# The scan's B held as three bf16 pieces and spread over the partitions by one bf16 product per state

## The chip, the cores and the metric

The kernel runs on one core of a Trainium2 chip. The metric is the time of one launch on the device in microseconds (us); lower is better. Several executions are timed, and one more is recorded by the hardware profiler.

## The reference, cut to what matters

The program is a two-layer network on x of shape (8, 512, 256) in float32. Each layer normalises x and adds two branches to it. In layer 0 the branches are a Mamba block (a selective state-space scan) and an FFN whose activations and weights are rounded to four-bit values in blocks of 16; in layer 1 they are a block-sparse attention and a two-deep stack of local attention and FFN. The change concerns the Mamba block:

```python
u = silu(conv(x_in) + conv_b)                        # (batch, 512 tokens, 512 channels)
x_dbl = einsum('bld,ed->ble', u, W_xproj)            # 16 + 16 + 16 columns
delta_raw, B_ssm, C_ssm = x_dbl[..., :16], x_dbl[..., 16:32], x_dbl[..., 32:]
delta = softplus(einsum('blr,dr->bld', delta_raw, W_dt) + b_dt)
def step(h, inp):                                    # over the tokens
    d_t, u_t, B_t, C_t = inp
    h = exp(d_t[:, :, None] * A) * h + (d_t * u_t)[:, :, None] * B_t[:, None, :]
    return h, einsum('bdn,bn->bd', h, C_t)           # 16 states n
```

Then y = ys + D u is gated with silu(z) and projected back to 256 columns. B at one token and one state is a single number which all 512 channels need.

## The kernel before, in words

The kernel has two stages, one for each layer, and the second begins when the first is over. In both, channels lie on the 128 partitions and the 512 tokens of one batch along them, so that a token scan is one VectorE (DVE) instruction along a row. NC = 4 groups of 128 channels make up the 512 channels, NS = 16 is the number of states, KC = 2 the groups of the 256 model columns, NB = 8 the batches.

The first stage is built from generators. `head(b)` (L251) loads and normalises a batch, turns it with TensorE (PE), runs the input projection and the convolution (L264 to L275), projects u to the 48 rows of delta, B and C (`ps_xp`, L279), copies them from PSUM to the tile `xd` with ScalarE (ACT, L283), writes the 16 rows of C to DRAM (L285), and forms delta and du = delta * u (L294 to L305: one PE product, four ACT operations, two DVE operations and three GpSimd (POOL) operations for each group of channels). `ffn(b)` (L309) is the four-bit FFN: rounding in `fp4` (L81 to L109), gate and up products (L330, L336), the turn of the hidden rows (`inner_to_partitions`, L191) and the down product (L350).

`scan(b)` (L356) is the recurrence. For each half of the channels (two groups, c0) and each of the 16 states n it does one step:

- a DMA from SP's queue spreads C's row n over the partitions (`cb`, L363, three buffers);
- a PE product spreads B's row n over the partitions: `sel[:, n, :]` has ones in row 16 + n and zeros elsewhere, so that `sel.T @ xd` repeats that row of `xd` 128 times in PSUM (`bb`, L366, pool `pb` of two buffers);
- for each of two channel groups: hh = du * bb (DVE, L369), da = exp(delta * A) (ACT, L374), the scan along the tokens (DVE, L376), hh * cb (POOL, L377), and a PE product with the identity that adds hh to `y` in PSUM over the 16 states (L378).

After the 16 states, z is projected and gated (L384 to L393), and after both halves the output projection (L399) and the sum (L403) close the batch.

`beside` (L111) interleaves the steps of `scan(b)` with those of `ffn(b)` and `head(b + 1)`; the first batch also carries the rounding of the weights and two tables. This gives the order in which the program is written. A scheduler of the framework then orders the instructions of each engine at compile time, by costs of its own, and within an engine the order is fixed when the program runs. Buffers that rotate (`rot`: `h` six, `cb` three; `pmm`, `pb`, `pda` two each in PSUM) set how far one engine may run ahead of another.

`sel` is made once at the start by 16 DVE copies of a column of the identity (L176 to L179), and `w_xp` and `w_dt` are loaded at L165 and L166.

Of the kernel before, what the change touches and what calls it, by code (L numbers as in the profile page):

```python
# [9 lines left out]
FP = mybir.dt.float32  # L10
BF = mybir.dt.bfloat16
AF = mybir.ActivationFunctionType
ALU = mybir.AluOpType
# [4 lines left out]
P = 128  # L18
NB, L, D = 8, 512, 256
NT = L // P  # L20
KC = D // P
DI, NS, DR = 512, 16, 16
NC = DI // P
# [7 lines left out]
DEPTH = 2  # L31
HID = 682
NHC = (HID + P - 1) // P
EPS = 1e-5
MASKED = -1e30

# [2 lines left out]
def tile_kernel(ctx: ExitStack, tc: tile.TileContext, a: dict, out: bass.AP):  # L39
    nc = tc.nc  # L40
    pe, dve, act, pool, sp = nc.tensor, nc.vector, nc.scalar, nc.gpsimd, nc.sync
# [87 lines left out]
    ident = const.tile([P, P], FP, name="ident")  # L129
# [4 lines left out]
    def load(p, src, shape, name, eng=sp):  # L134
        t = p.tile(shape, FP, name=name)
        eng.dma_start(t, src)
        return t

    def chunks(w):
        return w.rearrange("(k p) n -> p k n", p=P)  # L140
# [4 lines left out]
    with ExitStack() as s0:  # L145
        w0 = s0.enter_context(tc.tile_pool(name="w0", bufs=1))
        w1 = s0.enter_context(tc.tile_pool(name="io0", bufs=2))
# [14 lines left out]
        w_in = load(w0, chunks(a["w_in"]), [P, KC, 2 * DI], "w_in")  # L162
        conv_w = load(w0, a["conv_w"], [P, NC, 4], "conv_w")
        conv_b = load(w0, a["conv_b"], [P, NC], "conv_b")
        w_xp = load(w0, chunks(a["w_xp"]), [P, NC, DR + 2 * NS], "w_xp")  # L165
        w_dt = load(w0, a["w_dt"], [DR, DI], "w_dt")  # L166
        b_dt = load(w0, a["b_dt"], [P, NC], "b_dt")
        a_neg = load(w0, chunks(a["a_log"]), [P, NC, NS], "a_neg")
        d_par = load(w0, a["d_par"], [P, NC], "d_par")
# [2 lines left out]
        dve.tensor_scalar(a_neg, a_neg, -1.0, None, ALU.mult)  # L172


        sel = w0.tile([DR + 2 * NS, NS, P], FP, name="sel")
        for n in range(NS):  # L176
            dve.tensor_copy(
                sel[:, n, :], ident[: DR + 2 * NS, DR + n : DR + n + 1].to_broadcast([DR + 2 * NS, P])
            )  # L179


        w_g = w0.tile([P, KC, FI], FP, name="w_g")
# [66 lines left out]
        made = {}  # L249

        def head(b):  # L251
            x = load_x(b)
            xn = w1.tile([P, NT, D], FP, tag="xn", name="xn")
            layernorm(x, xn, sm)
            xt = w1.tile([P, KC, L], FP, tag="xt", name="xt")
            to_channels(xn, xt, pmm, "mm")
            yield


            u = w1.tile([P, NC, L], FP, tag="u", name="u")  # L260
            for c in range(NC):
                ps = pmm.tile([P, L], FP, tag="mm", name="ps_in")
                for k in range(KC):
                    pe.matmul(  # L264
                        ps, w_in[:, k, c * P : (c + 1) * P], xt[:, k, :], start=(k == 0), stop=(k == KC - 1)
                    )
                cv = rot.tile([P, L], FP, tag="t0", name="cv")
                dve.tensor_scalar(
                    cv, ps, conv_w[:, c, 3:4], conv_b[:, c : c + 1], ALU.mult, ALU.add
                )  # L270
                for s in range(1, 4):
                    dve.scalar_tensor_tensor(
                        cv[:, s:], ps[:, : L - s], conv_w[:, c, 3 - s : 4 - s], cv[:, s:], ALU.mult, ALU.add
                    )
                act.activation(u[:, c, :], cv, AF.Silu)  # L275
                yield
            ps = pmm.tile([P, L], FP, tag="mm", name="ps_xp")
            for c in range(NC):
                pe.matmul(  # L279
                    ps[: DR + 2 * NS, :], w_xp[:, c, :], u[:, c, :], start=(c == 0), stop=(c == NC - 1)  # L280
                )
            xd = w1.tile([DR + 2 * NS, L], FP, tag="xd", name="xd")
            act.copy(xd, ps[: DR + 2 * NS, :])  # L283
            c_d = dram.tile([NS, L], FP, tag="c_d", name="c_d")
            sp.dma_start(c_d, xd[DR + NS :, :])  # L285
            yield

            delta = w1.tile([P, NC, L], FP, tag="delta", name="delta")  # L290
            du = w1.tile([P, NC, L], FP, tag="du", name="du")
            for c in range(NC):
                ps = pmm.tile([P, L], FP, tag="mm", name="ps_dt")
                pe.matmul(ps, w_dt[:, c * P : (c + 1) * P], xd[:DR, :], start=True, stop=True)  # L294
                e = rot.tile([P, L], FP, tag="t0", name="e")
                w = rot.tile([P, L], FP, tag="t1", name="w")
                act.activation(e, ps, AF.Abs, bias=b_dt[:, c : c + 1])
                act.activation(delta[:, c, :], ps, AF.Relu, bias=b_dt[:, c : c + 1])
                act.activation(e, e, AF.Exp, scale=-1.0)
                dve.tensor_scalar(w, e, 1.0, None, ALU.add)  # L300
                dve.scalar_tensor_tensor(e, w, 1.0, e, ALU.subtract, ALU.subtract)
                act.activation(w, w, AF.Ln)
                pool.tensor_tensor(w, w, e, ALU.subtract)
                pool.tensor_tensor(delta[:, c, :], delta[:, c, :], w, ALU.add)
                pool.tensor_tensor(du[:, c, :], delta[:, c, :], u[:, c, :], ALU.mult)  # L305
                yield
            made[b] = x, xn, xt, u, xd, c_d, delta, du

        def ffn(b):  # L309

# [44 lines left out]

        def scan(b):  # L356

            x, xn, xt, u, xd, c_d, delta, du = made[b]
            for c0 in range(0, NC, 2):
                ys = [py.tile([P, L], FP, tag=f"y{i}", name=f"y{i}") for i in range(2)]  # L360
                for n in range(NS):
                    cb = rot.tile([P, L], FP, tag="cb", name="cb")
                    sp.dma_start(cb, c_d[n].unsqueeze(0).to_broadcast([P, L]))  # L363

                    bb = pb.tile([P, L], FP, tag="bb", name="bb")
                    pe.matmul(bb, sel[:, n, :], xd, start=True, stop=True)  # L366
                    hs = [rot.tile([P, L], FP, tag="h", bufs=6, name="hh") for i in range(2)]
                    for i in range(2):
                        dve.tensor_tensor(hs[i], du[:, c0 + i, :], bb, ALU.mult)  # L369
                    for i in range(2):  # L370
                        c = c0 + i

                        da = pda.tile([P, L], FP, tag="da", name="da")
                        act.activation(da, delta[:, c, :], AF.Exp, scale=a_neg[:, c, n : n + 1])  # L374
                        hh = hs[i]
                        dve.tensor_tensor_scan(hh, da, hh, 0.0, ALU.mult, ALU.add)  # L376
                        pool.tensor_tensor(hh, hh, cb, ALU.mult)  # L377
                        pe.matmul(ys[i], ident, hh, start=(n == 0), stop=(n == NS - 1))  # L378
                    yield
                for i in range(2):  # L380
                    c = c0 + i
                    ps = pmm.tile([P, L], FP, tag="mm", name="ps_z")
                    for k in range(KC):
                        pe.matmul(  # L384
                            ps, w_in[:, k, DI + c * P : DI + (c + 1) * P], xt[:, k, :],
                            start=(k == 0), stop=(k == KC - 1),
                        )
                    z = rot.tile([P, L], FP, tag="t1", name="z")
                    act.activation(z, ps, AF.Silu)
                    dve.scalar_tensor_tensor(  # L390
                        u[:, c, :], u[:, c, :], d_par[:, c : c + 1], ys[i], ALU.mult, ALU.add
                    )
                    pool.tensor_tensor(u[:, c, :], u[:, c, :], z, ALU.mult)  # L393
                yield
            xs = sums.pop(b)
            for t in range(NT):
                ps = pmm.tile([P, L], FP, tag="mm", name="ps_o")
                for c in range(NC):
                    pe.matmul(  # L399
                        ps[:, :D], u[:, c, t * P : (t + 1) * P], w_o[:, c, :],  # L400
                        start=(c == 0), stop=(c == NC - 1),
                    )
                dve.tensor_tensor(xs[:, t, :], xs[:, t, :], ps[:, :D], ALU.add)  # L403
            act.dma_start(x1_d[b], xs)
# [11 lines left out]
    with ExitStack() as s1:  # L416
        w0 = s1.enter_context(tc.tile_pool(name="w1", bufs=1, reuse_waits="tile"))
        w1 = s1.enter_context(tc.tile_pool(name="io1", bufs=2, reuse_waits="tile"))
# [40 lines left out]
        for j in range(4):  # L459
# [4 lines left out]
            "wqkv": [P, KC, 3 * IN], "tab": [P, 4, NT, LD], "wo": [P, IN // P, D],  # L464
            "wf1": [P, KC, 2 * HID], "wf2": [P, NHC, D],
        }
        lng, lnb, b1, b2c = [], [], [], []
        for l in range(DEPTH):
            lng.append(load(w0, a["lng"][l], [P, KC], f"lng{l}"))
            lnb.append(load(w0, a["lnb"][l], [P, KC], f"lnb{l}"))  # L470
            b1.append(load(w0, a["b1"][l], [P, 2, NHC], f"b1{l}"))
            b2c.append(load(w0, a["b2c"][l], [P, KC], f"b2c{l}"))
# [456 lines left out]
        for b in range(NB):  # L929
            more = b + 1 < NB  # L930
# [94 lines left out]
```

## Time and profile before

| | us |
|---|---|
| median of three runs | 4067.3 |
| the three runs | 4056.5, 4067.3, 4068.8 |
| the profiled execution | 4060.3 |
| its span, first to last instruction | 4058.3 |
| first stage | 0 to about 1722 |
| second stage | from there to the end |

Busy time in the whole span: PE 3690.3 us, DVE 2647.0 us, ACT 1724.7 us, POOL 1326.4 us. In the page, a group's row has the line of the kernel, the engine, the operation, what it writes and reads by the program's names, the shape, the count, then the busy time in us and the mean in ns of one, then the idle time of the engine just before the group's instructions and what ended most of it. PEld is PE's weight load, which may run beside a product. "PEclk" is the share of full speed that the PE clock was granted[...].

### The profile page before, as it was taken

How to read it: one execution, taken by the hardware profiler on the slowest of the kernel's cores; microseconds unless marked ns; L12 is line 12 of the kernel's file. 1: busy time of each engine (PE TensorE's matmuls, PEld its weight loads, DVE VectorE, ACT ScalarE, POOL GpSimd, SP SyncE). 2: the span in 40 equal slices, each digit the busy share in tenths (PEclk: the TensorE clock that was granted, in tenths of full speed). 3: DMA queues.
4: the chain of work that ended last, by engine and by line, in shares of the span. 5: the costliest groups of instructions: out<-in, count | busy, mean ns of one | idle time of the engine just before them, and what ended most of it. 6: DMA issues, size and time to landing. Idle time of an engine off the chain costs nothing.

```text
span 4058.3 us, 41394 instructions
## 1 busy us (share of the span) xinstructions
PE 3690.3 (91%) x14428; PEld 1757.7 (43%) x14444; DVE 2647.0 (65%) x4809; ACT 1724.7 (42%) x3411; POOL 1326.4 (33%) x1059
## 2 busy tenths in 40 slices
PE   5889898898988988989999999999999999999998
PEld 1334343434343434344553554544544445445545
DVE  7877879787978787765654555555455456456444
ACT  3454646455645555433343243244234234333333
POOL 4555556555655555521012012021111101201210
PEclk7788789888988888989999999999989999999999
DMA  2111111111111111120011011011101111100100
GB/s 84 45 39 47 45 47 50 44 47 44 47 47 46 49 39 47 60 88 27 27 53 42 14 56 43 20 45 43 38 27 43 38 40 34 53 27 27 48 27 6
DMA packets 88712, 171.96 MB, mean 42 GB/s; under 512 B 10024, under 2 KB 41768, under 8 KB 88504
## 3 DMA queue, kind: packets, MB, share of 16 engines
q1 hardware_dynamic: 85568, 162.95, 12.5%
q10 hardware_dynamic: 2936, 6.36, 0.4%
q8 instruction: 115, 1.88, 0.2%
q14 instruction: 93, 0.76, 0.1%
HBM read 159.58 MB, written 9.70 MB: 42 GB/s over the span
## 4 chain that ended last, share of the span: by engine, by line
PE 46%; DVE 7%; issue 2%; ACT 2%; POOL 1%; DMA 0%; SPq 0%; POOLq 0%; DVEq 0%; ACTq 0%
PE ps_qkv L707 8%; PE ps_g L877 5%; PE ps_a L877 4%; PE ps_wo L839 3%; PE ps_qk L538 3%; PE ps_y L912 2%; PE ps_w L895 2%; PE ps_st L633 2%; PE lo L811 2%; PE pt_qk L698 2%; PE ps_ls L759 2%; DVE pr L788 2%; PE pt L797 1%; DVE nm L769 1%; PE ps_s L583 1%
## 5 line engine op out<-in xcount | busy, mean ns | idle before, releaser
L377 POOL TENSOR_TENSOR hh<-hh,cb 128x512 f32<-128x512 f32 x512 | 660.3, 1302 | 452.3 <-PE y L378 116.8
L378 PE MATMUL y<-hh,ident 128*128 128x512 f32 x1024 | 640.5, 740 | 126.3 <-POOL hh L377 123.5
L376 DVE TENSOR_TENSOR_SCAN hh<-da,hh 128x512 f32<-128x512 f32 x512 | 604.9, 1206 | 11.2 <-ACT da L374 11.1
L374 ACT ACTIVATE da<-delta,a_neg 128x512 f32<-128x512 f32 x512 | 348.7, 689 | 441.1 <-DVE hh L376 439.6
L378 PEld LDWEIGHTS y<-hh,ident 128*128 128x128 f32 x1024 | 202.5, 223 | 460.1 <-POOL hh L377 341.7
L369 DVE TENSOR_TENSOR hh<-du,bb 128x512 f32<-128x512 f32 x512 | 333.9, 672 | 71.7 <-PE bb L366 63.1
L366 PE MATMUL bb<-xd,sel 48*128 48x512 f32 x512 | 311.0, 710 | 26.6 <-DVE hh L369 26.6
L775 ACT ACTIVATE pr<-ps_ls,nm 128x256 f32<-128x256 f32 (+1 forms) x512 | 221.8, 446 | 174.9 <-DVE nm L769 174.7
L726 POOL TENSOR_TENSOR r<-r,r 128x512 f32<-128x512 f32 x128 | 162.8, 1272 | 355.4 <-DVE r L724 355.4
L884 DVE SCALAR_TENSOR_TENSOR ht<-ps_a,b,gl 128x512 f32<-128x512 f32 x96 | 71.9, 749 | 252.1 <-PE ps_a L877 252.1
L487 POOL MEMSET sa<- 128x1 f32 x16 | 1.6, 102 | 711.9 <-DVE sa L843 384.6
L722 DVE TENSOR_TENSOR r<-ps_qkv,tab 128x512 f32<-128x512 f32 x128 | 87.9, 687 | 222.1 <-ACT sq L721 222.1
L883 ACT ACTIVATE gl<-ps_g,b 128x512 f32<-128x512 f32 x96 | 65.9, 686 | 379.4 <-PE ps_g L877 379.4
L877 PE MATMUL ps_g<-hn,wf 128*128 128x512 f32 (+1 forms) x384 | 207.6, 659 | 20.5 <-issue 20.4
L721 ACT ACTIVATE sq<-ps_qkv 128x512 f32<-128x512 f32 x128 | 76.6, 598 | 272.9 <-PE ps_qkv L707 272.9
L877 PE MATMUL ps_a<-hn,wf 128*128 128x512 f32 (+1 forms) x384 | 191.2, 618 | 0.0
L366 PEld LDWEIGHTS bb<-xd,sel 48*128 48x128 f32 x512 | 89.5, 207 | 234.6 <-DVE hh L369 94.6
L637 ACT ACTIVATE pt_e<-ps_st 128x512 f32<-128x512 f32 (+1 forms) x384 | 172.8, 536 | 14.6 <-PE ps_st L631 13.8
L769 DVE TENSOR_REDUCE nm<-ps_ls 128x2 f32<-128x512 f32 (+1 forms) x256 | 147.4, 617 | 43.4 <-PE ps_ls L759 42.6
L707 PE MATMUL ps_qkv<-wqkv,s 128*128 128x512 f32 x384 | 174.9, 605 | 0.0
L707 PE MATMUL ps_qkv<-wqkv,sf 128*128 128x512 f32 x384 | 173.3, 601 | 0.0
L788 DVE TENSOR_SCALAR pr<-pr,lrs 128x256 f32<-128x256 f32 (+1 forms) x512 | 148.6, 332 | 4.8
(213 smaller groups left out, 6622.1 us busy)
## 6 DMA issues: line engine op xcount, KB each, us to landing
cb<-c_d SPq DMA_DIRECT2D x256, 256.0 KB, 3.1
wqkv<-in_wqkv SPq DMA_DIRECT2D x16, 1536.0 KB, 6.2
wf<-in_wf SPq DMA_DIRECT2D x16, 1364.0 KB, 11.0
wf<-in_wf SPq DMA_DIRECT2D x16, 768.0 KB, 4.7
tab<-tab SPq DMA_DIRECT2D x18, 512.0 KB, 6.9
wo<-in_wo SPq DMA_DIRECT2D x16, 512.0 KB, 3.9
x<-in_x SPq DMA_DIRECT2D x8, 512.0 KB, 4.0
x<-xs ACTq DMA_DIRECT2D x8, 512.0 KB, 2.8
```

Of the source, the lines that this page charges most:

```text
L366: pe.matmul(bb, sel[:, n, :], xd, start=True, stop=True)
L369: dve.tensor_tensor(hs[i], du[:, c0 + i, :], bb, ALU.mult)
L374: act.activation(da, delta[:, c, :], AF.Exp, scale=a_neg[:, c, n : n + 1])
L376: dve.tensor_tensor_scan(hh, da, hh, 0.0, ALU.mult, ALU.add)
L377: pool.tensor_tensor(hh, hh, cb, ALU.mult)
L378: pe.matmul(ys[i], ident, hh, start=(n == 0), stop=(n == NS - 1))
L637: act.activation(pt[:, :n], banks[g][:, :n], AF.Exp)
L707: pe.matmul(ps, shifted(s, k, t * P, P), wqkv[:, k, i * IN : (i + 1) * IN], start=(k == 0), stop=(k == KC - 1),)
L769: dve.tensor_reduce(nm, banks[r][:, : 2 * nk].rearrange("p (g n) -> p g n", g=2), AX.X, ALU.max, negate=True)
L775: act.activation(pr[:, at], banks[r][:, at], AF.Exp, bias=nm[:, i : i + 1], accum_out=rs[:, i : i + 1],)
L788: dve.tensor_scalar(pr[:, at], pr[:, at], rs[:, i : i + 1], None, ALU.mult)
L877: pe.matmul(dst[:m], wf1[:, k, off + c * P : off + c * P + m], hn[:, k, :], start=(k == 0), stop=(k == KC - 1),)
```

## The change

The projection `w_xp` is widened on the host from 48 to 128 columns: B's 16 columns stand three times, at rows 0, 64 and 96 of its product, delta's at row 32, C's at row 48. In `head`, `xd` becomes the whole 128-row product in float32, and a bf16 tile `bp` gets its first rounding. Then for rows from 64 on, and again for rows from 96 on, the rounding is subtracted from `xd` on POOL and the rest is rounded into `bp` on ACT. After that the rows at 0, 64 and 96 of `bp` hold three bf16 pieces whose sum is B. `sel` is bf16, with ones at rows n, 64 + n and 96 + n, so that one product adds the three pieces and spreads the sum. The dt product and C's DMA read their rows at their new places. `scan` takes `bp` in the place of `xd`.

```diff
+RD, RC, PIECES = 32, 48, (0, 64, 96)
...
-        w_xp = load(w0, chunks(a["w_xp"]), [P, NC, DR + 2 * NS], "w_xp")
-        w_dt = load(w0, a["w_dt"], [DR, DI], "w_dt")
+        w_xp = load(w0, chunks(a["w_xp"]), [P, NC, P], "w_xp")
+        w_dt = w0.tile([RD + DR, DI], FP, name="w_dt")
+        sp.dma_start(w_dt[RD:, :], a["w_dt"])
...
-        sel = w0.tile([DR + 2 * NS, NS, P], FP, name="sel")
+        sel = w0.tile([P, NS, P], BF, name="sel")
+        every = w0.tile([P, NS], BF, name="every")
+        dve.tensor_copy(every, ident[:, :NS])
+        for at in PIECES[1:]:
+            dve.tensor_tensor(every, every, ident[:, at : at + NS], ALU.add)
         for n in range(NS):
-            dve.tensor_copy(
-                sel[:, n, :], ident[: DR + 2 * NS, DR + n : DR + n + 1].to_broadcast([DR + 2 * NS, P])
-            )
+            dve.tensor_copy(sel[:, n, :], every[:, n : n + 1].to_broadcast([P, P]))
...
             for c in range(NC):
-                pe.matmul(
-                    ps[: DR + 2 * NS, :], w_xp[:, c, :], u[:, c, :], start=(c == 0), stop=(c == NC - 1)
-                )
-            xd = w1.tile([DR + 2 * NS, L], FP, tag="xd", name="xd")
-            act.copy(xd, ps[: DR + 2 * NS, :])
+                pe.matmul(ps, w_xp[:, c, :], u[:, c, :], start=(c == 0), stop=(c == NC - 1))
+            xd = w1.tile([P, L], FP, tag="xd", name="xd")
+            act.copy(xd, ps)
             c_d = dram.tile([NS, L], FP, tag="c_d", name="c_d")
-            sp.dma_start(c_d, xd[DR + NS :, :])
+            sp.dma_start(c_d, xd[RC : RC + NS, :])
+
+            bp = w1.tile([P, L], BF, tag="bp", name="bp")
+            act.copy(bp, ps)
+            for at, more in ((PIECES[1], True), (PIECES[2], False)):
+                pool.tensor_tensor(xd[at:, :], xd[at:, :], bp[at:, :], ALU.subtract)
+                act.copy(bp[at:, :], xd[at:, :])
             yield
...
-                pe.matmul(ps, w_dt[:, c * P : (c + 1) * P], xd[:DR, :], start=True, stop=True)
+                pe.matmul(ps, w_dt[RD:, c * P : (c + 1) * P], xd[RD : RD + DR, :], start=True, stop=True)
...
-            made[b] = x, xn, xt, u, xd, c_d, delta, du
+            made[b] = x, xn, xt, u, bp, c_d, delta, du
...
-            x, xn, xt, u, xd, c_d, delta, du = made[b]
+            x, xn, xt, u, bp, c_d, delta, du = made[b]
...
-                    pe.matmul(bb, sel[:, n, :], xd, start=True, stop=True)
+                    pe.matmul(bb, sel[:, n, :], bp, start=True, stop=True)
...
+    w_xp, xp = i["L0_attn_W_xproj"].T, np.zeros((DI, P), f)
+    xp[:, RD : RD + DR], xp[:, RC : RC + NS] = w_xp[:, :DR], w_xp[:, DR + NS :]
+    for at in PIECES:
+        xp[:, at : at + NS] = w_xp[:, DR : DR + NS]
...
-        "w_xp": i["L0_attn_W_xproj"].T,
+        "w_xp": xp,
```

## The prediction

> **What bounds the kernel now.** I read the busy shares by stage first, because the change touches only the first stage (0 to 1722 us; the last output product of its scan ends there and the second stage begins).
>
> ```profile
> 0.00:1722.00 1722.00, 1496.20 (x3419) 626.64 (x3420) 1397.35 (x1989) 904.11 (x1178) 972.16 (x763) 0.86 0.16 48
> 1024.00:1033.00 9.00, 8.78 (x27) 4.45 (x26) 6.82 (x10) 7.46 (x9) 4.99 (x4) 1.00 0.16 44
> 1066.00:1080.00 14.00, 11.94 (x22) 3.59 (x20) 14.00 (x20) 7.89 (x10) 5.68 (x5) 0.90 0.07 20
> 1690.00:1712.00 22.00, 20.73 (x41) 6.33 (x40) 21.57 (x25) 8.78 (x13) 15.02 (x13) 1.00 0.26 72
> ```
>
> Columns: stretch, length, busy us of PE, PEld, DVE, ACT, POOL, then the granted PE clock. In the whole stage PE is busy 87% and DVE 81%: neither is full. The three short stretches say why. In 1024:1033 (gate and up products of the FFN) PE is full and DVE 76%; in 1066:1080 (convolution beside the scan) DVE is 100% and PE has gaps; in 1690:1712 (scan nearly alone) DVE is 98%. The bound alternates. The groups tell what the scan step costs each engine:
>
> ```profile
> L377 POOL TENSOR_TENSOR hh<-hh,cb 128x512 f32<-128x512 f32 x512 | 660.3, 1302 | 452.3 <-PE y L378 116.8
> L378 PE MATMUL y<-hh,ident 128*128 128x512 f32 x1024 | 640.5, 740 | 126.3 <-POOL hh L377 123.5
> L376 DVE TENSOR_TENSOR_SCAN hh<-da,hh 128x512 f32<-128x512 f32 x512 | 604.9, 1206 | 11.2 <-ACT da L374 11.1
> L369 DVE TENSOR_TENSOR hh<-du,bb 128x512 f32<-128x512 f32 x512 | 333.9, 672 | 71.7 <-PE bb L366 63.1
> L366 PE MATMUL bb<-xd,sel 48*128 48x512 f32 x512 | 311.0, 710 | 26.6 <-DVE hh L369 26.6
> ```
>
> There are 256 steps (8 batches, 2 halves, 16 states), yet bb has x512 and y x1024: one float32 product is two matmul instructions. DVE waits for bb itself only 63.1 us. The row of bb alone, with its waits:
>
> ```profile
> L366 PE MATMUL bb<-xd,sel x512: 589/589/1220, 43.6 to 1708.9; 48*128 48x512 f32 x171
> who waited for it (us, times):
>   POOL hh L377: 70.3, 31
>   DVE hh L369: 63.1, 48
> ```
>
> The median 589 ns is a record with its latency; the timeline has four of them in 1.98 us at full clock, so they follow each other at (1.98 - 0.589)/3 = 0.46 us. Records reach 1220 ns when the clock is halved. The page's chain of waits goes back only to about 1682 us (PE 46% of the span, nearly all second stage). I followed the stage's own waits further back by the same rule, from 1722 to 98 us: of 1624 us PE has 662, DVE 520, "issue" 160, POOL 141, ACT 106, and **bb 118.5**, y 267.
>
> [...]the granted clock is 1 or 0.5, its stretches in this stage are multiples of 3.41 us, and 495 of 1722 us are at half. [...]The trace of before has one such form, the bf16 mask product of the second stage, with a mean record of 391 ns[...].
>
> **The change, part by part.**
>
> *bb in one bf16 product (L366).* A float32 product takes two instructions at about 0.43 to 0.46 us, that is 0.88 us; the bf16 one 0.216[...]. It saves 0.66 us at full clock, 1.3 at half; at the stage's clock of 0.86, 0.77 us, times 256 = 197 us of PE time. That is not the gain. On the chain bb holds 118.5 us, and shrinking it takes off at most 118.5 x (1 - 0.39/1.12) = 77 us: 1.12 us is the pair in the timeline, 0.39 one bf16 record. Since the end is the longest of many paths, a shorter bb can only uncover others: 77 is the upper bound with this order and this clock. What is late next is DVE. When PE is full, DVE is busy 74 to 77% (below), so it takes over only after a fifth of the time is gone, while PE's work falls by about 197/1496 = 13%. But in the fullest stretches (1024:1033) no bb runs at all, and its relief there comes only from a PE queue that arrives earlier. I take 0.7 of the bound, **-54 us**; ends: -25 (a third, only half of the direct wait of 63 us gone) and -77.
>
> *The clock.* [...]I cut the stage into its 3.41 us windows and took PE's streaming share and DVE's busy share in each. Of 343 full-clock windows after 100 us 65 were followed by half clock: 38 of the 49 with a streaming share below 0.6, 15 of 69 between 0.6 and 0.8, one of 218 above. Shares 14% lower move windows down these bins; with the same rate per bin I count about 97 drops instead of 65, and half-clock windows go from 29% to some 38% of the stage, 45 more. Their price: DVE is busy 0.83 on average in half-clock windows against 0.81 in the others, so nothing is lost on average; but in the 32 of them where PE streams over 0.9, DVE is at 0.66, 0.19 of the pace or 0.63 us a window lower. Between 0 and 45 x 0.63 = 28 us; I take the middle, **+14 us**.
>
> *Order.* The scheduler orders by costs of its own. The compiled order of PE differs in about 350 lines of some 8460, mostly y against bb; of DVE in about 790 of 4810; of SP in a few cb and x loads that move by up to six places. No operation is lost. ACT gets 21 more table loads. I take no gain and no loss from the order, **0, within +-20 us**: each half of a step is 3.4 us on DVE, so 20 us is six displaced steps.
>
> *The split into pieces (L278 to L286), per batch.* ACT: the copy of xd now 128 partitions high (578 ns before at 48[...]), and three more copies at 0.58 us; POOL: two subtractions at about 1.3 us (row of L377). Eight batches: ACT 24 x 0.58 = 14 us plus 21 x 1.283 = 27 us, POOL 16 x 1.3 = 21 us. ACT works 904 of 1722 us and is on the chain for 106, a weight of 0.12; POOL 972 and 141, 0.15. So 41 x 0.12 + 21 x 0.15 = **+8 us**; ends 0 and 62. Queued behind them: on ACT the exps of da (for which the scan waits 11.1 us now), on POOL the products hh, for which y waits 123.5 us now. The new wait is bb's for bp: the first bb of the next batch stands on PE ahead of the last ps_dt and two or more pairs of y. Its cover is the time from ps_xp to there, about four scan steps or 14 us, against 4 x 0.58 + 2 x 1.3 = 5 us of chain and perhaps two foreign hh on POOL; if that cover went, it would cost some 5 us a batch, 40 us. dt reads other rows of xd and the compiled order shows it waiting for ACT alone.
>
> *Projection (L279), dt (L294), C (L285).* Same columns, same records[...]: 0. The DMA of C has the same 32 KB: 0.
>
> *Start.* w_xp is 256 KB instead of 96 (160 KB at the 380 GB/s that the first transfers reach is 0.4 us); sel is 16 copies at 264 ns before, 3.1 us on DVE, now bf16 on 128 rows, with three small operations of 0.2 us ahead: **+1 us**, ends -2 and +3, no cover since they are on the opening chain.
>
> Sum: -54 + 14 + 0 + 8 + 1 = **-31 us**. The profiled execution took 4060.3 us (span 4058.3), so 4029. The runs before have a median of 4067.3, 7 us above; I put the forecast halfway, **4033 us**. A difference of 0.3% (12 us) is about what can be told from none.
>
> **Rivals.**
>
> *R1, PE was the bound more than the chain says:* all of 77 us, no price of the clock, and an order that suits the shorter bb (-20): 4060 - 77 - 20 + 9 = 3972. For it: PE 87% busy, DVE's other waits on PE (ps_i 25, ps_u 22, ps_o 17, y 14 us). Against it: the stretches with DVE at 98 and 100%. Chance 0.14.
>
> *R2, hidden:* DVE takes over at once and the added work eats the rest: -25 + 14 + 8 = -3, so 4060. For it: 63 us of direct wait only, and none of the fullest PE stretches holds a bb. Chance 0.18.
>
> *R3, slower[...].* In the scan alone a step takes DVE 3.43 us (timeline at 1700); PE streams 3 x 0.88 = 2.6 us of it now, 77%, and 0.22 + 1.76 = 2.0 after, 58%, under the 0.6 where most windows drop. At half clock the two y alone take 3.5 us, as long as DVE's step, and PE must then also make up the FFN's products. If in addition the chance to recover falls from 0.45 to 0.35, half clock rises to 44%, 72 more windows, 45 us; with -25 for bb, +8, and +1 it is +29: 4090. It decides from a granted clock of about 0.79 in the stage (0.86 now). For it: 495 us at half clock already. Against it: DVE's pace in half-clock windows is not lower today. Chance 0.18.
>
> That the change doesn't do what it says: the compiled program has one bf16 matmul with its own weight load for each bb, so this is out.
>
> **How the numbers follow.** Forecast 0.50, R1 0.14, R2 0.18, R3 0.18. Faster: R1 and nearly all of the forecast, 0.62; same 0.20; slower 0.18. The forecast's own range is 3990 to 4055; to leave out no more than 2 in 10 I go to the edge of R1 and nearly all of R3: 3975 to 4090.
>
> **What would show it.** bb x256 with records near 0.4 us and PE's busy time in the stage down by 170 us or more; DVE's wait for bb below 30 us; DVE at 83% or more of a first stage that ends near 1690 us; a granted clock near 0.82. Wrong if DVE's share stays at 81% (the relief went nowhere), if the clock is under 0.79 and y's mean over 800 ns (R3), or if the stage ends before 1650 us (R1). The second stage should stay at 2336 us.

## The result, and the profile after

| | before | changed |
|---|---|---|
| median, us | 4068.1 (4 runs) | 4014.7 (4 runs) |
| lowest to highest, us | 4056.5 to 4071.0 | 3997.4 to 4020.3 |
| profiled execution, us | 4060.3 | 4020.3 |
| its span, us | 4058.3 | 4018.5 |

The ratio is 0.9867 with a 95% interval of 0.9831 to 0.9903, 53 us between the medians; a second group of runs of the same changed kernel gave 0.9889 (0.9864 to 0.9914). The forecast was 4033 us.

The gain lies in the first stage. The stretches of the changed kernel, columns as before (length, then busy us of PE, PEld, DVE, ACT, POOL, then the granted PE clock):

```profile
0.00:1682.00 1682.00, 1273.46 (x3127) 583.80 (x3166) 1407.72 (x1993) 943.50 (x1223) 993.52 (x779) 0.86 0.17 49
1682.00:4018.50 2336.50, 2194.73 (x11008) 1132.15 (x11024) 1249.54 (x2820) 821.31 (x2233) 354.16 (x296) 0.95 0.11 38
```

The second stage takes 2336.5 us, against 2336.3 before. The first ends 40 us earlier. PE lost 223 us of busy time there (records of 38 bb products are missing from this trace, which makes up at most some 14 us of it), DVE has about what it had (1408 us, now 84% of the stage), and the mean clock is the same 0.86. The rows of the step, from the page:

```profile
L387 PE MATMUL y<-hh,ident 128*128 128x512 f32 x1024 | 631.5, 725 | 217.7 <-POOL hh L386 215.5
L385 DVE TENSOR_TENSOR_SCAN hh<-da,hh 128x512 f32<-128x512 f32 x512 | 604.3, 1205 | 2.6 <-ACT da L383 2.5
L378 DVE TENSOR_TENSOR hh<-du,bb 128x512 f32<-128x512 f32 x512 | 332.2, 671 | 55.7 <-PE y L387 35.2
```

PE now waits 215.5 us for POOL before y, where it waited 123.5: it has become early. The row of bb itself (218 of its 256 records are in the trace):

```profile
L375 PE MATMUL bb<-bp,sel x218: 376/379/634, 47.1 to 1670.3; 128*128 128x512 bf16 x109
who waited for it (us, times):
  POOL hh L386: 105.7, 22
  DVE hh L378: 10.6, 6
```

One record of 379 ns stands where a pair of 1.12 us stood. Near the end of the stage the timeline has

```profile
1659.27 0.38 PE L375 MATMUL bb<-bp,sel 128*128 128x512 bf16 x1
1659.48 0.59 PE L408 MATMUL ps_o<-w_o,u 128*128 128x256 f32 x2
```

The product behind bb starts 0.21 us after it, so bb holds PE for 0.21 us. The prediction's 0.216 us, an assumption when it was made, agrees with that. The trace of before has the same distance in a bf16 pair of its second stage, two records of 0.38 us (the group's median is 379 ns) in 0.59 us at full clock:

```profile
1967.95 0.59 PE L752 MATMUL ps_ls<-mask,identb 128*128 128x512 bf16 x2
```

DVE's wait for bb fell from 63.1 to 10.6 us.

What DVE waited for, longest first, in the first stage and its last sums. The kernel before:

```profile
DVE h L341 <- ACT h L340: 80.6, 34, 3.3
DVE hh L369 <- PE bb L366: 63.1, 48, 4.2
DVE w L300 <- ACT e L299: 26.4, 15, 6.0
DVE ht L50 <- PE ps_i L191: 25.5, 20, 3.5
DVE h L341 <- PE ps_u L336: 22.2, 15, 2.5
```

and the changed kernel:

```profile
DVE h L350 <- PE ps_u L345: 42.7, 24, 4.3
DVE h L350 <- ACT h L349: 40.7, 18, 3.3
DVE hh L378 <- PE y L387: 35.2, 33, 3.7
DVE xs L412 <- PE ps_o L408: 30.9, 14, 6.5
DVE u L399 <- PE y L387: 29.4, 27, 3.0
```

DVE's waits sum to 322 us before and 271 after. Those that PE ended did not shrink (165 and 180 us): the wait for bb went, others on PE took its place. Those that ACT ended fell from 139 to 74 us; the largest, of h on ACT's silu, halved, while h's wait for PE's up product rose from 22.2 to 42.7 us.

### The profile page after: what moved, and what is told of

It reads as the page before. It is cut to its first block, busy times and chain, and to the rows that moved or that the text cites. A ratio compares the mean times of both kernels' runs of the same rounds, so it can differ in the third digit from the quotient of the medians.

```text
span 4018.5 us, 40903 instructions
## 1 busy us (share of the span) xinstructions
PE 3468.2 (86%) x14134; PEld 1716.0 (43%) x14188; DVE 2657.3 (66%) x4812; ACT 1764.8 (44%) x3456; POOL 1347.7 (34%) x1075
## 4 chain that ended last, share of the span: by engine, by line
PE 46%; DVE 8%; issue 2%; ACT 2%; POOL 1%; DMA 0%; SPq 0%; POOLq 0%; DVEq 0%; ACTq 0%
PE ps_qkv L716 8%; PE ps_g L886 5%; PE ps_a L886 4%; PE ps_wo L848 3%; PE ps_qk L547 3%; PE ps_y L921 2%; PE ps_w L904 2%; PE ps_st L642 2%; PE lo L820 2%; PE pt_qk L707 2%; PE ps_ls L768 2%; DVE pr L797 2%; PE pt L806 1%; DVE nm L778 1%; PE ps_s L592 1%
## 5 line engine op out<-in xcount | busy, mean ns | idle before, releaser
L387 PE MATMUL y<-hh,ident 128*128 128x512 f32 x1024 | 631.5, 725 | 217.7 <-POOL hh L386 215.5
L778 DVE TENSOR_REDUCE nm<-ps_ls 128x2 f32<-128x512 f32 (+1 forms) x256 | 147.4, 617 | 45.4 <-PE ps_ls L768 44.5
L383 ACT ACT_TABLE_LOAD x123 | 157.8, 1283 | 2.2
L768 PE MATMUL ps_ls<-lkt,lqt 64*128 64x256 f32 (+1 forms) x1024 | 140.2, 396 | 1.0
```

The source lines that it names most:

```text
L768: pe.matmul(banks[r][:, i * nk : (i + 1) * nk], qt[LD * r : LD * (r + 1), 2 * p + i, w * P : (w + 1) * P], kt[LD * r : LD * (r + 1), 2 * p ...
L778: dve.tensor_reduce(nm, banks[r][:, : 2 * nk].rearrange("p (g n) -> p g n", g=2), AX.X, ALU.max, negate=True)
```

## The experiments

My theory was the prediction's: the time comes from PE's shorter bb, and the clock, the order and the split add and take away little. The rivals: the order did it; the clock moves with PE's load; PE's time is not what decides. Each experiment was timed in five rounds beside the kernel before on the same chip, and its ratio is to those runs. The experiments ran in three groups on three chips; `split_f32_48`, `split_f32_128`, `bf16_rows16` and `no_split` form one, the changed kernel's second timing, `bb_once`, `dose2` and `dose4` another, the rest the third. Between groups the ratios are compared, and 0.001 is 4 us.

**The split without its bf16 product** (`split_f32_48`): the changed kernel, with bb in float32 again.

```diff
-        sel = w0.tile([P, NS, P], BF, name="sel")
+        sel = w0.tile([48, NS, P], FP, name="sel")
...
-            dve.tensor_copy(sel[:, n, :], every[:, n : n + 1].to_broadcast([P, P]))
+            dve.tensor_copy(sel[:, n, :], ident[:48, n : n + 1].to_broadcast([48, P]))
...
-                    pe.matmul(bb, sel[:, n, :], bp, start=True, stop=True)
+                    pe.matmul(bb, sel[:, n, :], xd[:48, :], start=True, stop=True)
```

> The projection with B three times, the split into pieces and all its ScalarE and GpSimd work stay as in the changed kernel, but bb is again a float32 product, over the 48 rows 0 to 47 of xd, whose first 16 hold B. If the gain is TensorE time taken from bb (my theory), this kernel keeps the cost of the split and loses the gain: 8 us above the kernel before, between 0 and 25. If the gain came from the scheduler's new order or from the wider projection, it should stand below the kernel before, by 20 us or more. Granted clock in the first stage about 0.86.

Measured: 4070.6 us, ratio 1.0018 (1.0010 to 1.0026), some 7 us slower than before. The wide projection, the split and the order made for them gain nothing; the gain comes with bb's product. From here to the changed kernel it is 52 to 61 us by the two ratios of that kernel. The scheduler's order changes in this step too, so the order that goes with the bf16 product isn't excluded here.

**The same over 128 rows** (`split_f32_128`): 128 in the place of each 48 above. If the granted clock follows streaming time alone, clock and time stay as with 48 rows.

> The same, but the float32 product of bb runs over all 128 rows of xd (the other rows meet zeros in sel). The products take as many columns as over 48 rows, and the engines' order is the same but for a few instructions at the start. [...]as the windows of the traces of before and after suggest (a window keeps or gets full clock from 0.37 of 128 rows all the time), the clock of the first stage rises from 0.86 to about 0.95 and the time falls below that of the 48 rows by 10 to 30 us.

Measured: 4020.2 us, ratio 0.9896 (0.9877 to 0.9915). This was the turn of the study. A float32 product, as long in columns as before, brings nearly all that the bf16 product brings. The stage of the two kernels (columns as above), first 48 rows:

```profile
0.00:1729.50 1729.50, 1496.22 (x3420) 636.34 (x3421) 1407.45 (x1989) 914.10 (x1198) 1002.32 (x779) 0.85 0.16 48
```

then 128 rows:

```profile
0.00:1684.80 1684.80, 1369.64 (x3420) 620.73 (x3421) 1402.52 (x1989) 913.15 (x1198) 1003.55 (x779) 0.92 0.17 49
```

The counts on every engine are the same; the clock is 0.92 instead of 0.85, and with it PE is busy 127 us less. The granted clock differs with the rows alone.

**The kernel before, with 128 rows** (`before_rows128`), the cleanest form of the same: no split, no bf16, every engine's order unchanged.

```diff
-        sel = w0.tile([DR + 2 * NS, NS, P], FP, name="sel")
+        sel = w0.tile([P, NS, P], FP, name="sel")
...
-            xd = w1.tile([DR + 2 * NS, L], FP, tag="xd", name="xd")
-            act.copy(xd, ps[: DR + 2 * NS, :])
+            xd = w1.tile([P, L], FP, tag="xd", name="xd")
+            act.copy(xd, ps)
...
-        "w_xp": i["L0_attn_W_xproj"].T,
+        "w_xp": padded(i["L0_attn_W_xproj"].T, 1, P),
```

> The kernel before with one thing changed: xd and sel are 128 rows high instead of 48 (the projection's 80 further columns are zero), so that bb's float32 product runs over 128 rows. Every engine has the same instructions in the same order. [...]the first stage's clock rises from 0.86 to 0.92 or more and the time falls by 40 to 60 us, as far as the changed kernel's or further, with no bf16 at all. If what helped the float32 product over 128 rows before was something else than the rows, it stays within 10 us of the kernel before.

Measured: 4017.3 us, ratio 0.9884 (0.9868 to 0.9900), 50 us faster: the changed kernel's time. Its stage, the rows of bb and y from its page, and bb's records:

```profile
0.00:1680.50 1680.50, 1380.70 (x3420) 620.31 (x3421) 1395.88 (x1989) 904.05 (x1178) 975.83 (x763) 0.92 0.17 49
```

```profile
L364 PE MATMUL bb<-xd,sel 128*128 128x512 f32 x512 | 283.1, 657 | 31.4 <-DVE hh L367 31.2
L376 PE MATMUL y<-hh,ident 128*128 128x512 f32 x1024 | 595.8, 686 | 189.0 <-POOL hh L375 183.7
L364 PE MATMUL bb<-xd,sel x512: 592/592/1223, 43.7 to 1666.9; 128*128 128x512 f32 x171
```

bb's mean is 657 ns instead of 710, y's 686 instead of 740, and only the clock did it: the medians at full clock are 592 ns for bb over 128 rows and 589 over 48. The stage is at half clock for 276 us instead of 495.

With dt over 128 rows as well (`before_rows128_dt128`; w_dt padded with zeros and `xd` in the place of `xd[:DR, :]`):

> The same, and the dt product too runs over 128 rows instead of 16 (w_dt is zero in the others). Four float32 products per batch more are counted, 27 us of TensorE's streaming in the stage. By the count of rows times columns the clock rises by another 0.01 to 0.02, and the time falls by a further 2 to 10 us; by the rival nothing moves.

Measured: 4016.9 us, ratio 0.9885 (0.9868 to 0.9902). The profiled stage had a clock of 0.93, but the time did not move by anything that the intervals show; they can't tell the lower end of what I expected, 2 us, from nothing.

**The changed kernel over 16 rows** (`bf16_rows16`), the rows taken away on the bf16 side, same order:

```diff
-                    pe.matmul(bb, sel[:, n, :], bp, start=True, stop=True)
+                    pe.matmul(bb, sel[:16, n, :], bp[:16, :], start=True, stop=True)
```

> The changed kernel with bb's bf16 product over the first 16 rows alone, so that B's second and third piece are left out of the sum; the split is still made, and the order of all engines is that of the changed kernel. [...]more half-clock windows, the clock of the first stage falls by about 0.03 (from 0.87 to 0.84 by my count), and the time rises by 5 to 20 us.

Measured: 4025.5 us, ratio 0.9914 (0.9891 to 0.9937). Its stage:

```profile
0.00:1691.00 1691.00, 1305.47 (x3165) 574.50 (x3165) 1405.26 (x1993) 943.32 (x1223) 993.91 (x779) 0.84 0.16 49
```

The clock is 0.84, where the changed kernel has 0.86 and 0.85 in its two profiles. Over the whole of each timed execution it is 0.902 to 0.911 in these six and 0.910 to 0.922 in the changed kernel's ten, so the clock did fall. The time is of the expected sign and size (10 to 19 us by the ratios), but the intervals overlap; what the lower clock cost isn't settled by this pair.

**Four and two bf16 products** (`dose4`, `dose2`), with sel divided by their number:

```diff
...
+            dve.tensor_scalar(sel[:, n, :], sel[:, n, :], 1.0 / 4, None, ALU.mult)
...
-                    pe.matmul(bb, sel[:, n, :], bp, start=True, stop=True)
+                    for j in range(4):
+                        pe.matmul(bb, sel[:, n, :], bp, start=(j == 0), stop=(j == 4 - 1))
```

> Four bf16 products for each bb, with sel quartered: as much TensorE time at full clock as the float32 product of the kernel before, over 128 rows. If the product's time is all that the change gained, this stands at the kernel before plus the split, 4070 us. [...]it stands where the float32 product over 128 rows stood, ratio 0.990, 4015 to 4030 us, at a clock of about 0.92 in the first stage.

Measured: 4024.9 us, ratio 0.9906 (0.9882 to 0.9931), stage clock 0.91. As much PE work as float32 has, over 128 rows (1376 us busy in the stage, against 1370), and the time of `split_f32_128`: there is no sign that bf16 as such has a part in it.

> Two bf16 products for each bb, with sel halved, which add up to the same sum: 55 us more TensorE work at full clock. If TensorE's work decides, 10 to 25 us slower than the changed kernel. If the clock decides (my count gives 0.90 for the first stage, from 0.87), it pays for itself: within 8 us of the changed kernel either way.

Measured: 4038.5 us, ratio 0.9949 (0.9932 to 0.9966), stage clock 0.88. Two products are slower than one, as PE's work says, but also slower than four, which neither theory says. The scheduler made a different order for each (the two differ on all engines), so I take it that a dozen us between kernels of different order can be the order's; that was not isolated.

The changed kernel again, in that group:

> The changed kernel as it is, beside the three others of this group on the same chip: ratio 0.987 to the kernel before, some 53 us.

Measured: 4016.2 us, ratio 0.9889 (0.9864 to 0.9914), 45 us.

**Without the split** (`no_split`): the loop over the two further pieces is gone, and sel has its ones at row n only.

```diff
-            for at, more in ((PIECES[1], True), (PIECES[2], False)):
-                pool.tensor_tensor(xd[at:, :], xd[at:, :], bp[at:, :], ALU.subtract)
-                act.copy(bp[at:, :], xd[at:, :])
...
-        for at in PIECES[1:]:
-            dve.tensor_tensor(every, every, ident[:, at : at + NS], ALU.add)
```

> The changed kernel without the two subtractions and the two further roundings per batch: bp is B rounded once to bf16, the second and third piece are left out. This removes 16 ScalarE and 16 GpSimd operations. If the split costs what the prediction said (8 us, of which the copies and subtractions are some 4), this is 2 to 10 us faster than the changed kernel; if the new wait of bb for bp had no cover, 30 to 40 us faster.

Measured: 4000.3 us, ratio 0.9848 (0.9831 to 0.9866). By the ratios that is 8 to 17 us below the changed kernel, with intervals that overlap: at the upper end of what I expected or above it, and below the 30 to 40 of an uncovered wait. The order differs here too, and DVE waits 44.5 us for bb where it waited 10.6. Its stage:

```profile
0.00:1658.40 1658.40, 1256.30 (x3165) 573.20 (x3165) 1399.72 (x1991) 929.06 (x1203) 976.28 (x763) 0.88 0.17 50
```

With dt over 128 rows (`no_split_dt128`):

> The changed kernel without the split (B rounded once to bf16, the second and third piece left out), and with the dt product over 128 rows. The order is that of the kernel without the split but for a few instructions. By my count the clock rises from 0.894 to 0.898 only, so the time is 0 to 5 us below the kernel without the split, whose ratio to the kernel before was 0.985.

Measured: 4003.4 us, ratio 0.9847 (0.9826 to 0.9867): no difference.

**y in bf16 as well** (`no_split_y_bf16`), to see whether a still lighter PE helps:

```diff
...
-                        pool.tensor_tensor(hh, hh, cb, ALU.mult)
-                        pe.matmul(ys[i], ident, hh, start=(n == 0), stop=(n == NS - 1))
+                        hb = rot.tile([P, L], BF, tag="hb", bufs=6, name="hb")
+                        pool.tensor_tensor(hb, hh, cb, ALU.mult)
+                        pe.matmul(ys[i], identh, hb, start=(n == 0), stop=(n == NS - 1))
```

> The changed kernel without the split, and with the 512 products of y in bf16 too (h times C is rounded to bf16 by GpSimd, which is left out of float32): 330 us less TensorE work at full clock, but as much less counted activity. If TensorE were still the bound and the clock stayed, DVE's 1400 us would be the next: 80 to 150 us faster than the kernel without the split. By the count of rows times columns the first stage falls to half clock for most of its length, a mean near 0.64, where the 620 us of work left take 970 us: TensorE is then not the bound over the stage but late in the FFN's stretches; 20 to 70 us faster than the kernel without the split. This is the place where the prediction's third rival would show, if it exists.

Measured: 3993.0 us, ratio 0.9824 (0.9804 to 0.9843); against `no_split` 7 to 10 us, with overlapping intervals. Its stage:

```profile
0.00:1657.00 1657.00, 1005.28 (x2625) 492.35 (x2655) 1391.71 (x1992) 892.88 (x1175) 975.61 (x763) 0.71 0.17 50
```

Against `no_split`, a fifth of PE's busy time is gone, the clock fell from 0.88 to 0.71, and the stage ends where it ended. I expected 20 to 70 us. The order differs too. That the lower clock took the gain was not separated from the order, nor from DVE and the waits around it having become the bound.

**One bb for 16 states** (`bb_once`):

```diff
-                    bb = pb.tile([P, L], FP, tag="bb", name="bb")
-                    pe.matmul(bb, sel[:, n, :], bp, start=True, stop=True)
+                    if n == 0:
+                        bb = pb.tile([P, L], FP, tag="bb", name="bb")
+                        pe.matmul(bb, sel[:, n, :], bp, start=True, stop=True)
```

> bb's bf16 product is made once for the 16 states of a half, 16 products of the changed kernel's 256; the products for the other 15 states are left out, and DVE reads the one bb again. If TensorE's time for bb were still worth something, this gains: 240 x 0.216 = 52 us less TensorE work, of which the chain of the changed kernel would give a third, 10 to 20 us. By the count of rows times columns the clock of the first stage falls from 0.87 to 0.83, which costs 10 to 15 us. Both together: within 10 us of the changed kernel. If bb's latency and its two buffers held the scan up, 30 us or more faster.

Measured: 3970.5 us, ratio 0.9772 (0.9744 to 0.9800), 46 us below the changed kernel. A miss. Making bb still holds 46 us, or the order does: here ACT has 242 table loads in the stage and not 285, at 1283 ns each (their mean in the changed kernel's trace) 55 us less of ACT. DVE's waits that ACT ended went from 76 to 46 us and those that PE ended from 177 to 131. Walking back along the waits of the changed kernel's stage, as the prediction did for the kernel before, I find only some 13 us of bb on the chain. So bb's own time is too little for 46 us, which points to the order or the two buffers of bb; these weren't told apart.

## Why the prediction was right, and where it was not

**What the granted clock followed.** The stretches of one granted clock in the traces of before and after are multiples of 3.41 us. In each window of that length in the first stage I summed the streaming time of the products (the time in which their columns run through PE, without latency: for 512 columns at full clock 0.43 us for a float32 instruction and 0.216 for a bf16 one, their distance back to back in the traces of before and after, and 0.85 and 0.43 at half clock), weighted with the clock and with rows in use over 128, as a share of the window. With this measure one limit, between 0.35 and 0.39 in the first stage of every trace of this study, tells the next window's clock: in the kernel before 11 of 473 windows fall on the wrong side, in `no_split_y_bf16` 2 of 453. With streaming time alone, as in the prediction, some 50 of 473 were misplaced in the kernel before, even with one limit after full-clock windows and another after half-clock ones. In the second stage the measure does less well: with a limit of 0.37 it misplaces 23 to 33 of some 670 windows in each trace. In this currency the old bb counts 0.86 us x 48/128 = 0.32 us, the new one 0.21, the float32 one over 128 rows 0.86 and bf16 over 16 rows 0.03. The sum and its limit are my reading of the traces; that rows matter is shown by `before_rows128` (0.92 against 0.86, at the same columns and order).

**bb in one bf16 product: -54 forecast.** The step from `split_f32_48` to the changed kernel is 52 to 61 us, but that it comes so near is in part luck. The step holds three terms of the prediction at once: the shorter product, the clock, since the new product also fills 128 rows, and the order; bb and the clock together were put at -40. With few rows on both sides, from `split_f32_48` to `bf16_rows16`, the step is 45 us, its order included. That lies under the bound of 77 us, as it should, and near the choice of 0.7. Common to all of these is that PE's busy time in us fell (below), and the change is only one way to shorten it. The four corners:

| bb | few rows | 128 rows |
|---|---|---|
| float32 | 1.0018 (48 rows) | 0.9896 |
| bf16 | 0.9914 (16 rows) | 0.9867 and 0.9889 |

With few rows bf16 is worth 1.0%, with 128 rows nothing that these intervals show. Either step takes PE's busy time of the stage from 1496 us to 1381 or below (1370 in `split_f32_128`, 1305 in `bf16_rows16`), and the stage ends between 1680 and 1691 us in all of these; the changed kernel's fall to 1273 brings no more. That fits the prediction's view that a shorter bb uncovers other paths, with the bend coming sooner than 0.7 says. `dose2` doesn't fit it: with 1303 us of PE its stage ends at 1703.5.

**The clock: +14 forecast, no loss seen.** This is the term that failed, in its count and in its price.

The count: I let bb's streaming time fall to a quarter (0.88 to 0.216 us), kept the old rate of drops for each share of streaming time, and expected half clock in 38% of the stage. It was 485 of 1682 us, 29%, as before (495 of 1722). Counting the windows of both traces again, the shares did move down as forecast: 127 full-clock windows lie below 0.6, where 64 did. But fewer of these drop, 67 of 127 against 46 of 64, and more half-clock windows recover, 73 of 129 against 62 of 131. Counted with rows, bb fell by a third only (0.32 to 0.21 us), since the change also filled PE's rows with B three times. The trace of before had the sign of it: 48*128 stood in the row that I quoted, and of its full-clock windows between 0.6 and 0.8 those that dropped have 0.23 to 0.37 when rows are counted, those that kept the clock 0.36 to 0.79. (The prediction's own bins are also miscounted: 38, 15 and 1 drops don't make 65, nor 49, 69 and 218 windows 343; the totals leave 49 of 56 for the lowest bin.)

The price: half clock was taken to cost nothing on average, and 0.31 us a window in the middle. Between the kernel before and `before_rows128`, with one order, 218 us less of half clock, 64 windows, go with a stage that is 41.5 us and a launch that is 50 us shorter: an estimate of 0.65 to 0.8 us a window. Had the 45 more windows come, they would have cost 29 to 36 us by this estimate. Two errors of the term, a wrong count and a price too low, thus pulled opposite ways.

**The split: +8 forecast.** `split_f32_48` is 7 us above before, its order included; `no_split` is 8 to 17 us below the changed kernel, its order included. Both fit 8, and neither measures it alone. The wait of bb for bp had its cover: PE waited once, 0.5 us, for bp. The 21 more table loads came (285 in the stage, 264 before, 1283 ns each in both traces).

**The order: 0 within 20.** Not isolated. `dose2` and `bb_once` suggest that it can be worth a dozen us or more. **Projection, dt, C, start:** the first xd came at 40.6 us, before at 41.0; the records of the projection have a median of 592 ns at full clock in both traces, those of dt 587; nothing to see.

**The sum, -31, fell short of -53** by the clock's 14 us and 8 more; the two groups of runs (-53 and -45) differ by as much, and from profile to profile it was -40.

**The signs.** bb's records (379 ns), PE's fall (223 us), DVE's wait for bb (10.6), its share (84%) and the stage's end (1682) were as said; the clock (0.86, not 0.82) was not. **The rivals.** R1's 3972 did not come: DVE's other waits on PE grew while the one for bb went. R2 is out, as is R3 for this kernel: a mean clock of 0.79 was not reached. Half of R3 is seen in `no_split_y_bf16`, where a lighter PE (1005 us busy against 1256) goes with a clock of 0.71 against 0.88; that the clock is what kept 250 us less of PE to a gain of 7 to 10 us is not shown.

## What to carry to other kernels

Before shortening a product that PE is late with, look at the granted clock and at the rows that the products use: in this kernel, padding one product from 48 to 128 rows, at the same columns and order, raised the clock from 0.86 to 0.92 and gave the same 50 us as turning it into bf16. Here two remedies for one wait added up to little more than either alone. A chain's share was a ceiling and not the gain: 118 us of bb on the chain gave at most 77 by hand and some 45 on the chip with few rows. And half clock had a price here, by the estimate above 0.65 to 0.8 us a window, though the engine behind PE looked no slower on average.

## What the runs showed of the hardware

The granted clock followed rows in use times streaming time, not time alone: float32 products over 48 and 128 rows take 589 and 592 ns at full clock, but the stages around them ran at mean clocks of 0.86 and 0.92 (kernel before and `before_rows128`; 0.85 and 0.92 in the pair with the split). In the first stage, windows of 3.41 us with a sum under about 0.37 were followed by half clock, with 11 of 473 exceptions in the kernel before. Streaming time alone did not tell it: in the kernel before 14 of 66 full-clock windows in which PE streamed for 60 to 80% of the time were followed by half clock.

Width was nearly free here: ACT's copy of 128 rows instead of 48 takes 586 ns instead of 578, `before_rows128` with its projection over 128 columns instead of 48 is 50 us faster and not slower, and the dt product over 128 rows instead of 16 left the ratio where it was (0.9885 and 0.9884).
